# A gated recurrent cell on one core: half B's candidate for half A's chunks made in half A's bank, ten passes a step

## The chip, the cores and the metric

The kernel runs on one core of one Trainium2 chip. The metric is the device time of one execution in microseconds. Before the change it is 1663.17 us, the median of three runs (1661.68 to 1664.26). The engines are TensorE (PE, with its weight loads shown as PEld), VectorE (DVE), ScalarE (ACT), GpSimd (POOL) and the DMA queues, here issued by SyncE (SP).

## What is computed

A recurrent cell runs over 512 steps for a batch of 8, with 512 inputs and 512 units, all in 32-bit floats, and its states are added to the input:

```
def step(h, x_t):
    fused = sigmoid(concatenate([x_t, h], -1) @ w_W + w_b)
    hidden_state, output_state = split(fused, 2, -1)          # r and z
    memory_state = x_t @ wx_W + wx_b + hidden_state * (h @ wh_W + wh_b)
    h_new = output_state * h + (1 - output_state) * tanh(memory_state)
    return h_new, h_new
out = x + states
```

Each step needs the state of the step before, so nothing can be batched over time on the side of h: three products of the state (r, z and the candidate's h @ wh_W, called hh here) and then two sigmoids, a tanh and the update. The products of x don't depend on the state and are made ahead.

## The kernel before

**Layout.** Unit u lies on partition 32j + p in chunk c: four quads j of 128 units, each in four chunks of 32. Chunks 0 and 1 are half A, chunks 2 and 3 half B. The state of a step is the stationary operand of a product (32 columns: 8 batch rows of this step and zeros for three others of its group of four steps), the weights are the moving one. One *pass* is one chunk of the state against one bank's weights: four matrix products, one for each quad j, in four 32-wide strips of the array. Each fp32 product shows as two MATMUL records, so a pass has eight.

**Banks.** Products are added into PSUM tiles: A (192 columns: hh, z, r of half A), B (128: r, hh of half B), C (64: z of half B), each in two copies for alternate groups of four steps, and two tiles `xp` for the x side. Four steps share a bank; the rows of the other steps keep the x side and the biases, which `spread` (L254) copies in on ScalarE ahead of each group, from `xs` by the columns in `XP` (L43).

**A step** (loop at L363). PE takes the passes in the order of the string `ORDER` (L27): A0 B0 A1 A2 A3 B1 B2 B3 C0 C1 C2 C3, the digit being the chunk of the state. Passes 0 and 1 need half A's new state, 2 and 3 half B's. Then comes one part of the x products of a group that lies ahead (`products`, L293; an eighth each step, as much as one pass of 384 columns in four steps of a group of eight and of 288 in the other four; they end 12 steps before the last). The first step has its own order `FIRST` (L29), in which half A's bank is `xp` itself.

**VectorE and ScalarE in a step** (L458 to L483), in this order on each engine's queue: for half A `turn_r`, `turn_h`, `turn_z` (32x32 transposes out of PSUM, with a sigmoid on ScalarE behind r and z), `memory(0, q)` (a scan that makes r * hh + x, with a tanh behind it, one for each chunk q); then `turn_r(1)`, `turn_h(1)`, `update(0, 0)`, `turn_z(1)`, `update(0, 1)`, `memory(1, q)`, `update(1, q)`. `update` is a scan that makes z * h + (1 - z) * n, the new state, which the next step's weight loads wait for. `memory` scans over slots: `md0` holds [0, r], `md1` holds [hh, x], so a unit has two elements and the second result is the one wanted. Behind these stand copies and adds for the x side, different in each step of a group of eight (L487 to L547), and two tiny memsets. GpSimd adds the state to the input.

The order on each engine is written by hand (`manual_schedule`, L186); what waits for what follows from the tiles, with a few manual dependencies: the second update of half A waits for the sigmoid of half B's r (L467).

**Start.** SP brings wx (four parts), wa (four parts, by chunk of the state), wb (chunks 0 to 2, then 3), then the inputs.

Of the kernel before, what the change touches and what calls it, by code (L numbers as in the profile page):

```python
# [25 lines left out]

ORDER = "A0 B0 A1 A2 A3 B1 B2 B3 C0 C1 C2 C3"  # L27

FIRST = "A0 x A1 x A2 x A3 B0 B1 B2 B3 C0 C1 C2 C3"  # L29

BANKS = {"A": 192, "B": 128, "C": 64}

HALF = 192
# [5 lines left out]
Q01, Q23 = slice(0, 64), slice(64, 128)  # L39

COLS = slice(64, 448)

XP = {"A": slice(0, 192), "X": slice(192, 320), "C": slice(320, 384), "B": slice(384, 512)}  # L43


@with_exitstack
def tile_cond_rnn_residual(
# [5 lines left out]
    wa_d: bass.AP,  # L53
    wb_d: bass.AP,
    wb3_d: bass.AP,
    bias_d: bass.AP,
# [30 lines left out]
    nc = tc.nc  # L87
# [4 lines left out]
    const = ctx.enter_context(tc.tile_pool(name="const", bufs=1))  # L92
# [38 lines left out]

    wa = const.tile([P, NQ, NQ, 192], F32, name="wa")
    for k in range(NQ):
        nc.sync.dma_start(out=wa[:, k], in_=wa_d[k])
    wb = const.tile([P, NQ, NQ, 192], F32, name="wb")
    nc.sync.dma_start(out=wb[:, :3], in_=wb_d)
    nc.sync.dma_start(out=wb[:, 3], in_=wb3_d)

    def wh(bank, k, j):
        return wa[:, k, j] if bank == "A" else wb[:, k, j, {"C": slice(0, 64), "B": slice(64, 192)}[bank]]  # L140
# [9 lines left out]
    NH = 2 * GS  # L150
    hT = [[pair(n, f"hT{n}{i}", 32, 3) for i in range(NH)] for n in "AB"]

    md0 = [[pair(n, f"md0{n}{i}", 32, 2) for i in range(2)] for n in "AB"]
    md1 = [[pair(n, f"md1{n}{i}", 32, 2) for i in range(2)] for n in "AB"]
    hd0 = [[pair(n, f"hd0{n}{i}", B, 3) for i in range(2)] for n in "AB"]
# [10 lines left out]
    nc.scalar.activation(const.tile([P, 1], F32, name="table"), zeros[:, :1], AF.Sigmoid)  # L166
    for n, t_ in enumerate(hd0[0] + hd0[1] + md0[0] + md0[1] + hT[0] + hT[1]):
# [7 lines left out]
    step_bias = const.tile([P, HALF], F32, name="stepbias")  # L175
    xs = [const.tile([P, 512], F32, name=f"xs{n}") for n in range(2)]
    u2 = const.tile([P, WIDE], F32, name="u2")
# [3 lines left out]
    def state(hf, i, slot=2):  # L181

        s = i % GS
        return hT[hf][i % NH][:, B * s : B * s + B, :, slot]
# [8 lines left out]
    def mm(out_, lhsT, rhs, start=False):  # L193
        nc.tensor.matmul(  # L194
            out_, lhsT, rhs, start=start, stop=False, skip_group_check=True
        )
# [13 lines left out]
    for t_ in xs:  # L210
        for c_ in (slice(0, 64), slice(448, 512)):
            nc.gpsimd.tensor_copy(t_[:, c_], bias[:, c_])
    for hf in range(2):
# [9 lines left out]
    def act(key, out_, in_, func, **kw):  # L223
        inst = nc.scalar.activation(out_, in_, func, **kw).ins  # L224
# [24 lines left out]

    def source(g):  # L250

        return xs[g % 2] if g else xps[0]

    def spread(g, names):  # L254

        for n in names:
            nc.scalar.copy(banks[g % 2][n], source(g)[:, XP[n]])

    def turn_x(g, e):

        c0 = XP["X"].start + 32 * e
        nc.vector.transpose(md1[e // 2][g % 2][:, :, e % 2, 1], source(g)[:, c0 : c0 + 32])

# [92 lines left out]
    weight_sum(0)  # L356
    spread(0, "BCA")
    for e in range(NQ):
# [4 lines left out]
    for i in range(T):  # L363
        g, s = divmod(i, GS)
        c, t = divmod(i, TC)
        ps = banks[g % 2]
# [21 lines left out]
        def scan(c_, out_, d0, d1):  # L388
# [23 lines left out]
        def turn_r(hf):  # L412
            tr, _ = turned("r", hf)
            r_done[hf] = act(
                ("r", hf, g % 2, s),
                md0[hf][g % 2][:, rows, :, 1].rearrange("p n c -> p c n"),
                tr,
                AF.Sigmoid,
            )

        def turn_h(hf):
            inst = nc.vector.transpose(  # L422
                md1[hf][g % 2][:, :, :, 0].rearrange("p n c -> p c n"), raw["h"][hf]
            ).ins
            h_done[hf] = inst
            if hf == 0 and i + 1 - NH in pool_done:
                tc.add_manual_dep(inst, pool_done[i + 1 - NH].name, SYNC)

        def turn_z(hf):
# [10 lines left out]
            )  # L440

        ms = [
            work.tile([P, 2, B, 2], F32, tag=f"m{hf}", name=f"m{hf}_{i}").rearrange("p c n s -> p n c s")
            for hf in range(2)
        ]

        def memory(hf, q):

            c_ = slice(q, q + 1)
            scan(c_, ms[hf], md0[hf][g % 2][:, rows], md1[hf][g % 2][:, rows])  # L450
            act(("n", hf, q, i % NH), state(hf, i, 1)[:, :, c_], ms[hf][:, :, c_, 1], AF.Tanh)
# [37 lines left out]
        if i == 0:  # L489
            nc.scalar.copy(xs[1][:, COLS], xps[1][:, COLS])  # L490
            spread(1, "B")
            turn_x(1, 0)
        add_ = nc.vector.tensor_tensor
        if u == 3 and o and nxt:
            add_(xs[0][Q23, COLS], xps[0][Q23, COLS], both[Q23], ALU.add)
        elif u == 7 and two:
            nc.vector.tensor_copy(xs[0][Q01, COLS], xps[0][Q01, COLS])
        elif u == 0 and o and nxt:
            add_(u3[Q23], xps[1][Q23, COLS], u2[Q23], ALU.add)
# [4 lines left out]
        if u == 0:  # L504
            spread(2 * o + 1, "C")
            if o and nxt:
                nc.scalar.copy(xps[0][Q01, lo], step_bias[Q01])
                nc.scalar.copy(xps[1][Q23, lo], step_bias[Q23])
        elif u == 1:
            spread(2 * o + 1, "A")  # L510
            if o == 0:
                seed(3)
        elif u == 2:
            if o == 0:
                nc.scalar.copy(xs[0][:, COLS], xps[0][:, COLS])
            elif nxt:
                nc.scalar.copy(both[Q23, HALF:], xps[0][Q01, lo])
                nc.vector.tensor_copy(both[Q23, :HALF], xps[1][Q23, lo])
            if two:
                nc.scalar.copy(xps[0][Q01, COLS], bias[Q01, COLS])  # L520
        elif u == 3:
            if o == 0:
                nc.scalar.copy(xs[1][:, COLS], xps[1][:, COLS])
            if two:
                x_sum(o + 2, 2)
        elif u == 4 and nxt:
            if o:
                add_(xs[1][Q01, COLS], xps[1][Q01, COLS], u3[Q23], ALU.add)
            spread(2 * o + 2, "A")
            if two:  # L530
                x_sum(o + 2, 0)
        elif u == 5 and nxt:
            if o:
                add_(xs[1][Q23, COLS], u3[Q23], both[Q23], ALU.add)
            if two:
                nc.scalar.copy(xps[0][Q23, COLS], xps[0][Q01, COLS])
                x_sum(o + 2, 1)
            spread(2 * o + 2, "C")
        elif u == 6 and nxt:
            spread(2 * o + 2, "B")  # L540
            if two:
                nc.vector.memset(xps[1][Q01, COLS], 0.0)
                x_sum(o + 2, 3)
        elif u == 7 and nxt:
            if two:
                nc.scalar.copy(u2[Q23], xps[0][Q23, COLS])
            spread(2 * o + 3, "B")  # L547
        if i < len(SUMS):
# [108 lines left out]
```

## Time and profile before

| | |
|---|---|
| median of the runs | 1663.17 us |
| profiled execution, first to last instruction | 1659.2 us |
| PE, share busy | 99% |
| PEld, share busy | 89% |
| DVE | 78% |
| ACT | 67% |
| POOL | 20% |
| granted clock of TensorE | 1.000 |

In a group line or a row of the timeline, `L194 PE MATMUL A<-wa,hTA 128*32 128x192 f32 x8` means: line 194 of the kernel, on PE, writes tile A from the weights wa and the state of half A (hTA); 128 by 32 is stationary, 128 by 192 moving; eight records. In brackets stands how long the engine was idle before, and which instruction ended that. The names on VectorE are tr, tz (transposed r and z), md1A and md1B (transposed hh), m (the scan behind tanh), hTA and hTB (the state). Busy time of PE is made of pipelined records whose ends are modelled; differences of starts tell more.

### The profile page before, as it was taken

The numbers are of one execution on the slowest core, as the hardware profiler recorded it, in microseconds if no ns is written. First come the engines' busy times: TensorE is split into PE (matmuls) and PEld (weight loads), VectorE is DVE, ScalarE is ACT, GpSimd is POOL, SyncE is SP. The second block draws the span as 40 slices with busy tenths as digits, with TensorE's granted clock in tenths as the row PEclk, the third lists the DMA queues.
The fourth block names the chain that finished last, engine by engine and source line by source line (L and its number), as shares of the span: only waits on it lengthen the run. The fifth ranks groups of instructions, "written<-read, shape, count | busy, mean of one in ns | idle before, by whom it ended". The sixth has DMA issues, their size and how long they took to land.

```text
span 1659.2 us, 126037 instructions
## 1 busy us (share of the span) xinstructions
PE 1647.1 (99%) x54254; PEld 1484.3 (89%) x54254; DVE 1298.5 (78%) x9702; ACT 1106.9 (67%) x5884; POOL 325.6 (20%) x1284
## 2 busy tenths in 40 slices
PE   8999999999999999999999999999999999999998
PEld 5899999999999888899999999988899999999997
DVE  6877777777777777777777777777777777777776
ACT  4666666666666666666666666666666666666665
POOL 2221121211211212112112121121121211211211
PEclk9999999999999999999999999999999999999999
DMA  4000000000000000000000000000000000000000
GB/s 180 17 5 18 17 18 18 17 6 18 17 17 18 5 18 18 18 18 5 18 18 18 18 12 10 18 17 18 18 5 18 17 18 18 5 17 11 11 11 10
DMA packets 11512, 31.16 MB, mean 19 GB/s; under 512 B 1220, under 2 KB 1732, under 8 KB 10824
## 3 DMA queue, kind: packets, MB, share of 16 engines
q1 hardware_dynamic: 10800, 22.94, 4.0%
q8 instruction: 424, 6.95, 1.8%
q14 instruction: 136, 1.11, 0.2%
q10 hardware_dynamic: 152, 0.16, 0.0%
HBM read 14.70 MB, written 8.39 MB: 14 GB/s over the span
## 4 chain that ended last, share of the span: by engine, by line
PE 98%; DMA 1%; DVE 1%; issue 0%; ACT 0%; SPq 0%
PE A L194 40%; PE B L194 26%; PE xp L194 18%; PE C L194 13%; DMA wb<-in_wb_dram 1%; DMA wx<-in_wx_dram 0%; DVE tr L406 0%; DVE m L390 0%; DVE tz L406 0%; DVE hTA L390 0%; DVE md1A L422 0%; DVE md1B L422 0%; ACT hTB L224 0%; SPq L130 0%; DVE hTB L390 0%
## 5 line engine op out<-in xcount | busy, mean ns | idle before, releaser
L194 PE MATMUL A<-wa,hTA 128*32 128x192 f32 x8176 | 555.5, 327 | 2.7 <-DVE hTA L390 2.7
L194 PE MATMUL B<-wb,hTA 128*32 128x128 f32 x8192 | 453.0, 273 | 0.9 <-DMA wb<-in_wb_dram 0.9
L194 PE MATMUL A<-wa,hTB 128*32 128x192 f32 x8176 | 446.6, 326 | 0.0
L194 PEld LDWEIGHTS A<-wa,hTA 128*32 128x32 f32 x8176 | 290.7, 122 | 128.4 <-DVE hTA L390 107.1
L558 POOL TENSOR_TENSOR ot<-xin,hTB 128x16 f32<-128x16 f32 x503 | 125.6, 250 | 1292.4 <-DVE hTB L390 1281.8
L194 PEld LDWEIGHTS B<-wb,hTA 128*32 128x32 f32 x8192 | 346.8, 122 | 10.8 <-DMA wb<-in_wb_dram 1.3
L194 PE MATMUL B<-wb,hTB 128*32 128x128 f32 x8192 | 338.6, 273 | 0.1
L194 PEld LDWEIGHTS A<-wa,hTB 128*32 128x32 f32 x8176 | 324.3, 122 | 15.5 <-DVE hTB L390 0.3
L224 ACT ACTIVATE md0A<-tr 128x16 f32<-128x16 f32 x512 | 112.3, 219 | 314.4 <-DVE tr L406 314.4
L406 DVE STREAM_TRANSPOSE tr<-A 128x64 f32<-128x64 f32 x511 | 127.7, 250 | 214.3 <-PE A L194 199.3
L194 PE MATMUL xp<-tw,sx 128*32 128x384 f32 x1984 | 274.2, 406 | 0.3 <-issue 0.3
L194 PEld LDWEIGHTS B<-wb,hTB 128*32 128x32 f32 x8192 | 261.1, 122 | 0.4 <-DMA wb<-in_wb_dram 0.4
L390 DVE TENSOR_TENSOR_SCAN hTB<-hd0B,hTB 128x24 f32<-128x24 f32 x1024 | 157.8, 195 | 100.5 <-ACT hTB L224 100.5
L194 PE MATMUL C<-wb,hTB 128*32 128x64 f32 x8192 | 230.0, 219 | 0.1
L194 PE MATMUL C<-wb,hTA 128*32 128x64 f32 x8192 | 229.1, 219 | 0.0
L194 PE MATMUL xp<-wx,xin 128*32 128x384 f32 x1056 | 210.1, 486 | 0.0
L194 PEld LDWEIGHTS C<-wb,hTA 128*32 128x32 f32 x8192 | 206.6, 122 | 0.0
L390 DVE TENSOR_TENSOR_SCAN hTA<-hd0A,hTA 128x24 f32<-128x24 f32 x1024 | 190.9, 186 | 0.0
L194 PEld LDWEIGHTS C<-wb,hTB 128*32 128x32 f32 x8192 | 179.5, 122 | 0.6 <-issue 0.4
L224 ACT ACTIVATE hd0B<-tz 128x16 f32<-128x16 f32 x512 | 115.7, 226 | 94.8 <-DVE tz L406 94.8
L224 ACT ACTIVATE hTB<-hTB 128x16 f32<-128x16 f32 x512 | 120.1, 235 | 79.2 <-DVE hTB L390 70.3
L224 ACT ACTIVATE hTA<-m 128x8 f32<-128x8 f32 x1024 | 160.8, 206 | 2.5
(98 smaller groups left out, 2710.0 us busy)
## 6 DMA issues: line engine op xcount, KB each, us to landing
xin<-in_x_dram SPq DMA_DIRECT2D x31, 256.0 KB, 3.3
out_dram<-ot SPq DMA_DIRECT2D x31, 256.0 KB, 2.1
wx<-in_wx_dram SPq DMA_DIRECT2D x4, 768.0 KB, 7.1
wa<-in_wa_dram SPq DMA_DIRECT2D x4, 384.0 KB, 9.1
wb<-in_wb_dram SPq DMA_DIRECT2D x1, 1152.0 KB
wb<-in_wb_dram SPq DMA_DIRECT2D x1, 384.0 KB, 11.2
out_dram<-ot SPq DMA_DIRECT2D x1, 192.0 KB, 2.1
head<-in_xh_dram ACTq DMA_DIRECT2D x1, 144.0 KB, 5.0
```

The lines of the kernel that those rows point to most:

```text
L194: nc.tensor.matmul(out_, lhsT, rhs, start=start, stop=False, skip_group_check=True)
L224: inst = nc.scalar.activation(out_, in_, func, **kw).ins
L390: return nc.vector.tensor_tensor_scan(*[t_[:, :, c_].rearrange("p n c s -> p (n c s)") for t_ in (out_, d0, d1)], 0.0, ALU.mult, ALU.add,).ins
L406: inst = nc.vector.transpose(t_.rearrange("p c n -> p (c n)"), raw[n][hf]).ins
L558: return engine.tensor_tensor(ot[:, t, 2 * hf : 2 * hf + 2, :].rearrange("p c n -> p n c"), x_of(c, slice(2 * hf, 2 * hf + 2), t, 1).rearr ...
```

## The change

The columns a step multiplies stay the same, but they lie in other banks. Bank A has 256 columns, of which the first 64 are hh of half B; for chunks 0 and 1 the pass takes all 256, for chunks 2 and 3 the last 192. Bank D (128) holds z and r of half B. Bank H (64) holds hh of half B for chunks 2 and 3 alone. So a step has ten passes. The two parts of hh of half B are added in the scan: `md1` of half B has three slots [part, H, x], `md0` of half B [0, 1, r], and `turn_part` is a new transpose on VectorE of A's first 64 columns. `update(0, 0)` moves ahead of `turn_h(1)`. Half A's first 64 columns start at zero, from a widened `xs`; biases and x parts move to the new columns.

```diff
-ORDER = "A0 B0 A1 A2 A3 B1 B2 B3 C0 C1 C2 C3"
-FIRST = "A0 x A1 x A2 x A3 B0 B1 B2 B3 C0 C1 C2 C3"
-BANKS = {"A": 192, "B": 128, "C": 64}
+ORDER = "A0 A1 A2 A3 D0 D1 D2 D3 H2 H3"
+FIRST = "A0 x A1 x A2 x A3 D0 D1 D2 D3 H0 H1 H2 H3"
+BANKS = {"A": 256, "D": 128, "H": 64}
...
-XP = {"A": slice(0, 192), "X": slice(192, 320), "C": slice(320, 384), "B": slice(384, 512)}
+XP = {"A": slice(0, 256), "X": slice(256, 384), "D": slice(384, 512), "H": slice(512, 576)}
...
-    wa = const.tile([P, NQ, NQ, 192], F32, name="wa")
+    wa = const.tile([P, NQ, NQ, 256], F32, name="wa")
...
-    wb = const.tile([P, NQ, NQ, 192], F32, name="wb")
-    nc.sync.dma_start(out=wb[:, :3], in_=wb_d)
-    nc.sync.dma_start(out=wb[:, 3], in_=wb3_d)
+    wd = const.tile([P, NQ, NQ, 128], F32, name="wd")
+    nc.sync.dma_start(out=wd[:, :3], in_=wd_d)
+    nc.sync.dma_start(out=wd[:, 3], in_=wd3_d)
...
+    for t_ in md0[1]:
+        nc.gpsimd.memset(t_[:, :, :, 1], 1.0)
...
             hs = hT[k // 2][i % NH][:, :, k % 2, 2]
+            to, w_ = {
+                "A": (ps["A"], wa) if k < 2 else (ps["A"][:, 64:], wa[:, :, :, 64:]),
+                "D": (ps["D"], wd),
+                "H": (ps["H"], wa[:, :, :, :64]),
+            }[bank]
+            if bank == "A" and i == 0:
+                to, w_ = xps[0][:, :HALF], wa[:, :, :, 64:]
             for j in range(NQ):
-                to = ps[bank] if i or bank != "A" else xps[0][:, XP["A"]]
-                mm(to[32 * j : 32 * j + 32, :], hs, wh(bank, k, j))
+                mm(to[32 * j : 32 * j + 32, :], hs, w_[:, k, j])
...
-        pa = ps["A"] if i else xps[0][:, XP["A"]]
+        pa = ps["A"][:, HU:] if i else xps[0][:, :HALF]
         raw = {
-            "h": (pa[:, :HU], ps["B"][:, HU:]),
-            "z": (pa[:, HU : 2 * HU], ps["C"]),
-            "r": (pa[:, 2 * HU :], ps["B"][:, :HU]),
+            "h": (pa[:, :HU], ps["H"]),
+            "z": (pa[:, HU : 2 * HU], ps["D"][:, :HU]),
+            "r": (pa[:, 2 * HU :], ps["D"][:, HU:]),
         }
...
+        def turn_part():
+            nc.vector.transpose(md1[1][g % 2][:, :, :, 0].rearrange("p n c -> p c n"), ps["A"][:, :HU])
+
         ms = [
-            work.tile([P, 2, B, 2], F32, tag=f"m{hf}", name=f"m{hf}_{i}").rearrange("p c n s -> p n c s")
+            work.tile([P, 2, B, 2 + hf], F32, tag=f"m{hf}", name=f"m{hf}_{i}").rearrange("p c n s -> p n c s")
...
         memory(0, 1)
+        if i:
+            turn_part()
         turn_r(1)
+        update(0, 0)
         turn_h(1)
-        update(0, 0)
         turn_z(1)
         tc.add_manual_dep(update(0, 1), r_done[1].name, SYNC)
...
         if u == 0:
-            spread(2 * o + 1, "C")
+            spread(2 * o + 1, "D")
...
-            spread(2 * o + 2, "C")
+            spread(2 * o + 2, "D")
         elif u == 6 and nxt:
-            spread(2 * o + 2, "B")
+            spread(2 * o + 2, "H")
...
-            spread(2 * o + 3, "B")
+            spread(2 * o + 3, "H")
```

More of the change, by code (lines that the diff above doesn't have):

```diff
@@ L41 @@
 COLS = slice(64, 448)
-XP = {"A": slice(0, 192), "X": slice(192, 320), "C": slice(320, 384), "B": slice(384, 512)}
+SC = slice(128, 512)
+XP = {"A": slice(0, 256), "X": slice(256, 384), "D": slice(384, 512), "H": slice(512, 576)}
 @with_exitstack
@@ L53, in tile_cond_rnn_residual @@
     wa_d: bass.AP,
-    wb_d: bass.AP,
-    wb3_d: bass.AP,
+    wd_d: bass.AP,
+    wd3_d: bass.AP,
     bias_d: bass.AP,
@@ L130, in tile_cond_rnn_residual @@
         nc.sync.dma_start(out=wx[:, k], in_=wx_d[k])
-    wa = const.tile([P, NQ, NQ, 192], F32, name="wa")
+    wa = const.tile([P, NQ, NQ, 256], F32, name="wa")
     for k in range(NQ):
         nc.sync.dma_start(out=wa[:, k], in_=wa_d[k])
-    wb = const.tile([P, NQ, NQ, 192], F32, name="wb")
-    nc.sync.dma_start(out=wb[:, :3], in_=wb_d)
-    nc.sync.dma_start(out=wb[:, 3], in_=wb3_d)
-    def wh(bank, k, j):
-        return wa[:, k, j] if bank == "A" else wb[:, k, j, {"C": slice(0, 64), "B": slice(64, 192)}[bank]]
+    wd = const.tile([P, NQ, NQ, 128], F32, name="wd")
+    nc.sync.dma_start(out=wd[:, :3], in_=wd_d)
+    nc.sync.dma_start(out=wd[:, 3], in_=wd3_d)
     load_x(0, 1)
@@ L151, in tile_cond_rnn_residual @@
     hT = [[pair(n, f"hT{n}{i}", 32, 3) for i in range(NH)] for n in "AB"]
-    md0 = [[pair(n, f"md0{n}{i}", 32, 2) for i in range(2)] for n in "AB"]
-    md1 = [[pair(n, f"md1{n}{i}", 32, 2) for i in range(2)] for n in "AB"]
+    md0 = [[pair(n, f"md0{n}{i}", 32, m) for i in range(2)] for n, m in (("A", 2), ("B", 3))]
+    md1 = [[pair(n, f"md1{n}{i}", 32, m) for i in range(2)] for n, m in (("A", 2), ("B", 3))]
     hd0 = [[pair(n, f"hd0{n}{i}", B, 3) for i in range(2)] for n in "AB"]
@@ L166, in tile_cond_rnn_residual @@
     nc.scalar.activation(const.tile([P, 1], F32, name="table"), zeros[:, :1], AF.Sigmoid)
-    for n, t_ in enumerate(hd0[0] + hd0[1] + md0[0] + md0[1] + hT[0] + hT[1]):
+    for n, t_ in enumerate(hd0[0] + hd0[1] + md0[0] + md0[1] + hT[0] + hT[1] + md1[1]):
         (nc.vector if n < DVE_FILL else nc.gpsimd).memset(t_, 0.0)
+    for t_ in md0[1]:
+        nc.gpsimd.memset(t_[:, :, :, 1], 1.0)
     for t_ in hd0[0] + hd0[1]:
@@ L175, in tile_cond_rnn_residual @@
     step_bias = const.tile([P, HALF], F32, name="stepbias")
-    xs = [const.tile([P, 512], F32, name=f"xs{n}") for n in range(2)]
+    xs = [const.tile([P, 576], F32, name=f"xs{n}") for n in range(2)]
     u2 = const.tile([P, WIDE], F32, name="u2")
@@ L210, in tile_cond_rnn_residual @@
     for t_ in xs:
-        for c_ in (slice(0, 64), slice(448, 512)):
-            nc.gpsimd.tensor_copy(t_[:, c_], bias[:, c_])
+        nc.gpsimd.memset(t_[:, :64], 0.0)
+        nc.gpsimd.tensor_copy(t_[:, 64:128], bias[:, :64])
+        nc.gpsimd.tensor_copy(t_[:, 512:], bias[:, 448:])
     for hf in range(2):
@@ L248, in prefill_two, with source @@
         yield from prefill(3)
-    def source(g):
-        return xs[g % 2] if g else xps[0]
+    def source(g, c0, c1):
+        return xs[g % 2][:, c0:c1] if g else xps[0][:, c0 - 64 : c1 - 64]
     def spread(g, names):
         for n in names:
-            nc.scalar.copy(banks[g % 2][n], source(g)[:, XP[n]])
+            skip = 64 if n == "A" and not g else 0
+            nc.scalar.copy(banks[g % 2][n][:, skip:], source(g, XP[n].start + skip, XP[n].stop))
     def turn_x(g, e):
         c0 = XP["X"].start + 32 * e
-        nc.vector.transpose(md1[e // 2][g % 2][:, :, e % 2, 1], source(g)[:, c0 : c0 + 32])
+        nc.vector.transpose(md1[e // 2][g % 2][:, :, e % 2, 1 + e // 2], source(g, c0, c0 + 32))
     def wx_of(kh, nh):
@@ L356, in tile_cond_rnn_residual @@
     weight_sum(0)
-    spread(0, "BCA")
+    spread(0, "HDA")
     for e in range(NQ):
@@ L415, in turn_r @@
                 ("r", hf, g % 2, s),
-                md0[hf][g % 2][:, rows, :, 1].rearrange("p n c -> p c n"),
+                md0[hf][g % 2][:, rows, :, 1 + hf].rearrange("p n c -> p c n"),
                 tr,
@@ L422, in turn_h @@
             inst = nc.vector.transpose(
-                md1[hf][g % 2][:, :, :, 0].rearrange("p n c -> p c n"), raw["h"][hf]
+                md1[hf][g % 2][:, :, :, hf].rearrange("p n c -> p c n"), raw["h"][hf]
             ).ins
@@ L450, in memory @@
             scan(c_, ms[hf], md0[hf][g % 2][:, rows], md1[hf][g % 2][:, rows])
-            act(("n", hf, q, i % NH), state(hf, i, 1)[:, :, c_], ms[hf][:, :, c_, 1], AF.Tanh)
+            act(("n", hf, q, i % NH), state(hf, i, 1)[:, :, c_], ms[hf][:, :, c_, 1 + hf], AF.Tanh)
         def update(hf, q):
@@ L489, in tile_cond_rnn_residual @@
         if i == 0:
-            nc.scalar.copy(xs[1][:, COLS], xps[1][:, COLS])
-            spread(1, "B")
+            nc.scalar.copy(xs[1][:, SC], xps[1][:, COLS])
+            spread(1, "H")
             turn_x(1, 0)
@@ L494, in tile_cond_rnn_residual @@
         if u == 3 and o and nxt:
-            add_(xs[0][Q23, COLS], xps[0][Q23, COLS], both[Q23], ALU.add)
+            add_(xs[0][Q23, SC], xps[0][Q23, COLS], both[Q23], ALU.add)
         elif u == 7 and two:
-            nc.vector.tensor_copy(xs[0][Q01, COLS], xps[0][Q01, COLS])
+            nc.vector.tensor_copy(xs[0][Q01, SC], xps[0][Q01, COLS])
         elif u == 0 and o and nxt:
@@ L514, in tile_cond_rnn_residual @@
             if o == 0:
-                nc.scalar.copy(xs[0][:, COLS], xps[0][:, COLS])
+                nc.scalar.copy(xs[0][:, SC], xps[0][:, COLS])
             elif nxt:
@@ L522, in tile_cond_rnn_residual @@
             if o == 0:
-                nc.scalar.copy(xs[1][:, COLS], xps[1][:, COLS])
+                nc.scalar.copy(xs[1][:, SC], xps[1][:, COLS])
             if two:
@@ L527, in tile_cond_rnn_residual @@
             if o:
-                add_(xs[1][Q01, COLS], xps[1][Q01, COLS], u3[Q23], ALU.add)
+                add_(xs[1][Q01, SC], xps[1][Q01, COLS], u3[Q23], ALU.add)
             spread(2 * o + 2, "A")
@@ L533, in tile_cond_rnn_residual @@
             if o:
-                add_(xs[1][Q23, COLS], u3[Q23], both[Q23], ALU.add)
+                add_(xs[1][Q23, SC], u3[Q23], both[Q23], ALU.add)
             if two:
@@ L626 @@
     wx_d = chunks(cat((z[:D], half_a), (r[:D], half_a), (wxm, both), (z[:D], half_b), (r[:D], half_b)))
-    wa_d = chunks(cat((whm, half_a), (z[D:], half_a), (r[D:], half_a)))
-    wb = units(cat((z[D:], half_b), (r[D:], half_b), (whm, half_b)))
-    wb_d, wb3_d = c_(wb[:, :3]), c_(wb[:, 3])
+    wa_d = chunks(cat((whm, half_b), (whm, half_a), (z[D:], half_a), (r[D:], half_a)))
+    wd = units(cat((z[D:], half_b), (r[D:], half_b)))
+    wd_d, wd3_d = c_(wd[:, :3]), c_(wd[:, 3])
     rb, zb = wb_[:512], wb_[512:]
@@ L643 @@
     for name, a in (
-        ("x", xd), ("xh", xh_d), ("wx", wx_d), ("wa", wa_d), ("wb", wb_d), ("wb3", wb3_d), ("bias", bias_d),
+        ("x", xd), ("xh", xh_d), ("wx", wx_d), ("wa", wa_d), ("wd", wd_d), ("wd3", wd3_d), ("bias", bias_d),
     ):
```

## The prediction

> **What bounds the kernel now.** I read the page first, then the table of waits, then the timeline of one ordinary step.
>
> ```profile
> span 1659.2 us, 126037 instructions
> PE 1647.1 (99%) x54254; PEld 1484.3 (89%) x54254; DVE 1298.5 (78%) x9702; ACT 1106.9 (67%) x5884; POOL 325.6 (20%) x1284
> ```
>
> ```profile
> PEld A L194 <- DVE hTA L390: 107.1, 379, 0.5
> ...
> PE A L194 <- DVE hTA L390: 2.7, 11, 0.3
> ```
>
> TensorE is busy throughout. Its weight loads wait 107 us for VectorE's new state, but its products only 2.7 us: the state arrives just in time, behind other products. So the time is the sum of the passes, plus whatever the state becomes late by. The passes, on PE (time of first start, length, count; a length overlaps the next, so I use differences of starts):
>
> ```profile
> 798.20 0.86 PE L194 MATMUL A<-wa,hTB 128*32 128x192 f32 x16
> 798.85 0.43 PE L194 MATMUL B<-wb,hTA 128*32 128x128 f32 x8
> 799.07 0.65 PE L194 MATMUL B<-wb,hTB 128*32 128x128 f32 x16
> 799.51 0.43 PE L194 MATMUL C<-wb,hTA 128*32 128x64 f32 x16
> 799.73 0.43 PE L194 MATMUL C<-wb,hTB 128*32 128x64 f32 x16
> 799.96 0.41 PE L194 MATMUL xp<-tw,xin 128*32 128x288 f32 x2
> ...
> 800.44 0.54 PE L194 MATMUL A<-wa,hTA 128*32 128x192 f32 x8
> 800.77 0.43 PE L194 MATMUL B<-wb,hTA 128*32 128x128 f32 x8
> 800.98 0.54 PE L194 MATMUL A<-wa,hTA 128*32 128x192 f32 x8
> 801.31 0.86 PE L194 MATMUL A<-wa,hTB 128*32 128x192 f32 x16
> ...
> 803.06 0.49 PE L194 MATMUL xp<-wx,xin 128*32 128x384 f32 x2
> ...
> 803.71 0.54 PE L194 MATMUL A<-wa,hTA 128*32 128x192 f32 x8
> ```
>
> Eight records are one pass. Two passes of 192 columns take 0.65 (798.20 to 798.85), so 0.325 each; four of 64 take 0.45 (799.51 to 799.96), so 0.1125 each; one of 128 takes 0.22. A line through these is 1.66 ns a column and 6 ns a pass. The x products at a step's end take 0.48 in a short step (799.96 to 800.44) and 0.65 in a long one (803.06 to 803.71).
>
> ```profile
> L194 PE MATMUL xp<-wx,sx 128*32 128x288 f32 x496 | 83.2, 406 | 0.0
> ```
>
> A group of eight steps has 8 such records, so there are 62 groups, and by `products` each has four short and four long steps: 248 of each. Around the same steps VectorE runs:
>
> ```profile
> 799.12 0.25 DVE L406 STREAM_TRANSPOSE tr<-A 128x64 f32<-128x64 f32 x1 [0.37 <-PE A L194]
> 799.29 0.21 DVE L422 STREAM_TRANSPOSE md1A<-A 128x64 f32<-128x64 f32 x1
> ...
> 799.85 0.23 DVE L406 STREAM_TRANSPOSE tr<-B 128x64 f32<-128x64 f32 x1
> 800.00 0.21 DVE L422 STREAM_TRANSPOSE md1B<-B 128x64 f32<-128x64 f32 x1
> 800.13 0.20 DVE L390 TENSOR_TENSOR_SCAN hTA<-hd0A,hTA 128x24 f32<-128x24 f32 x1
> 800.25 0.22 DVE L406 STREAM_TRANSPOSE tz<-C 128x64 f32<-128x64 f32 x1
> 800.39 0.17 DVE L390 TENSOR_TENSOR_SCAN hTA<-hd0A,hTA 128x24 f32<-128x24 f32 x1
> 800.48 0.25 DVE L390 TENSOR_TENSOR_SCAN m<-md0B,md1B 128x16 f32<-128x16 f32 x2
> 800.93 0.31 DVE L390 TENSOR_TENSOR_SCAN hTB<-hd0B,hTB 128x24 f32<-128x24 f32 x2 [0.20 <-ACT hTB L224]
> 801.27 0.56 DVE L495 TENSOR_TENSOR xs<-xp,both 64x384 f32<-64x384 f32 x1
> 801.87 0.21 DVE L262 STREAM_TRANSPOSE md1A<-xs 128x32 f32<-128x32 f32 x1
> 802.03 0.07 DVE L556 MEMSET idle<- 128x1 f32 x2
> 802.22 0.25 DVE L406 STREAM_TRANSPOSE tr<-A 128x64 f32<-128x64 f32 x1
> ```
>
> Bank A is finished at 798.85; its first transpose starts 0.27 later. From there half A's new state is due to A0 (scan 800.13, product 800.44), half B's to A2 (scan 800.93, product 801.31). What a late state costs stands at the end of the program, where 12 steps have no x product to wait behind; the first row is the load of A2's weights in the step above:
>
> ```profile
> 801.19 0.61 PEld L194 LDWEIGHTS A<-wa,hTB 128*32 128x32 f32 x16
> ...
> 1642.87 0.20 DVE L390 TENSOR_TENSOR_SCAN hTA<-hd0A,hTA 128x24 f32<-128x24 f32 x1
> ...
> 1643.13 0.19 PEld L194 LDWEIGHTS A<-wa,hTA 128*32 128x32 f32 x8 [0.39 <-DVE hTA L390]
> ```
>
> ```profile
> 1643.13 0.55 PE L194 MATMUL A<-wa,hTA 128*32 128x192 f32 x8 [0.24 <-DVE hTA L390]
> 1643.49 0.40 PE L194 MATMUL B<-wb,hTA 128*32 128x128 f32 x8
> ...
> 1646.21 0.55 PE L194 MATMUL A<-wa,hTA 128*32 128x192 f32 x8 [0.24 <-DVE hTA L390]
> ```
>
> The load starts 0.26 after its scan starts (1642.87, 1643.13). With nothing to hide it, the pass takes 0.36 (to 1643.49) and not 0.325: an uncovered load costs 0.04. In the ordinary short step A2's load comes 0.26 after the scan too (800.93, 801.19) and 0.12 ahead of its product. So half B has 0.12 - 0.04 = 0.08 us to spare in a short step and, with x products 0.17 longer, 0.25 in a long one.
>
> **The change part by part.** *Passes.* C0 and C1 go into A0 and A1; C0 to C3 and B0 to B3 become D0 to D3, H2 and H3. Columns a step stay 1536, passes fall from twelve to ten. At 6 ns a pass that is 12 ns a step, over 511 steps 6.1 us. The trace has no 256-column pass in 32-wide strips: bounded below by columns alone (0.425), above by a 192 and a 64 put together (0.4375); I take the line, 0.43.
>
> *VectorE's order.* Added: a transpose of A's first 64 columns, ahead of tr of half B. Transposes of this shape cost from start to next start 0.13 (800.00 to 800.13), 0.15 (799.85 to 800.00) or 0.17 (799.12 to 799.29). By the row that also writes md1B: 0.13. But r and z now share bank D, and D3 ends four 0.22 passes after A3, not three: tr of half B can't start before 0.87 + 0.27 after bank A's end, 0.87 after tr of half A, where it started 0.73 after it (799.12, 799.85). Both reasons give the same place, 0.13 to 0.14 later, so the floor is 0.14 even if the added transpose were free, and the ceiling 0.17. The scan of half A's state trades places with the second transpose, so it keeps its place (two transposes ahead of it before, two now): half A is due at A0 as before, 0.01 at risk. The transpose of H waits for H3, 0.87 + 0.22 = 1.09 after tr of half A; its place in the queue is 1.14, so no wait. Behind these stand z's transpose, the second scan of half A (needed at A1, now 0.43 after A0; it lands in time) and both m scans of half B, all 0.14 later.
>
> *Wider scans.* Half B's two m scans go from 16 to 24 elements. Two of 24 take 0.31 together (800.93), two of 16 0.25 (800.48), but one of 24 alone takes 0.17 (800.39). Bounds 0 to 0.05 on the way to tanh; I take 0.01.
>
> *Half B's deadline.* From A3's end to A2 there were ten passes and the x products, now eight: the two saved passes lie in this stretch, so A2 is due 0.012 earlier. Lateness: 0.14 + 0.01 + 0.012 - 0.08 = about 0.08 in a short step; I take 0.07, since a short step already holds some 0.01 of half A's waiting, which this one swallows. In a long step 0.25 - 0.16 = 0.09 is left: no stall.
>
> The Trainium skill, "TensorE: Matmul & The Clock Gate", section "LDWEIGHTS (loading the stationary operand)", puts a load at its columns divided by 1.2 in ns, an estimate of 27 ns for these 32 columns against the 0.04 of the rows above. By that rule each stall is 13 ns shorter and the sum below 3.2 us lower, 1674.0. The rows decide here.
>
> *Sum.* Stalls 248 x 0.07 = +17.4. Passes -6.1. In one short step of each group an add of 0.56 and a transpose stand between half B's scans and the next tr of half A, as at 801.27 to 802.22; 800.93 to 802.22 is 1.29 against A2-bound 0.26 + 0.04 + 0.65 + 0.27 = 1.22. That row waits for bank A almost as long itself, so I take 0.02 of the 0.07: 62 x 0.02 = +1.2. At the end 11 steps go from 3.08 (1643.13 to 1646.21, half A's loop) to half B's loop, 0.27 + 1.81 + 0.15 + 0.30 + 0.65 = 3.18: +1.1, and the 0.1 counted for their passes comes back: +1.2. Start-up:
>
> ```profile
> 17.88 0.66 PE L194 MATMUL B<-wb,hTA 128*32 128x128 f32 x16 [0.93 <-DMA wb<-in_wb_dram]
> ```
>
> ```profile
> 1.16 6.45 DMA wx<-in_wx_dram
> 7.63 11.19 DMA wb<-in_wb_dram
> ```
>
> The queue brings 6144 KB of weights by 18.8, about 350 KB a us. The first recurrent pass outside A waited for 1536 + 1152 KB behind wx; now for 2048 + 768, 128 KB more: +0.3. Scalar copies into the banks widen for A by 64 columns and swap 64 and 128 elsewhere; they lie behind ScalarE's wait:
>
> ```profile
> 799.40 0.22 ACT L224 ACTIVATE md0A<-tr 128x16 f32<-128x16 f32 x1 [0.16 <-DVE tr L406]
> ```
>
> That is the fullest step, with 0.16 left; half B's shift takes 0.15, the later tr gives 0.07 back: nothing, and at most 0.1 in one step of eight (6 us) if this cover fails. GpSimd's adds end no chain. In all +17.4 - 6.1 + 1.2 + 1.2 + 0.3 = +14.0: 1659.2 + 14.0 = 1673.2 in the profile's span. The median of the runs, 1663.17, lies 4.0 above that span: 1677.2.
>
> **The rivals.** (1) *Half B's state stays in time*: only the passes count, 1663.2 - 6.1 + 0.3 = 1657.4. For it: VectorE idles 0.37 ahead of tr (799.12), and ScalarE has room. Against: that idle lies behind half B's scans, not ahead of them. It decides from a lateness under 0.025 a short step (6.1 / 248). Chance 0.11. (2) *The stall is there but nearly paid for*: the load hides itself (0.04 off), 0.03 a stall, 7.4 - 6.1 + 2.7 = +4.0 at the most, +1.6 if the end and the adds cost nothing: 1665 to 1667. Chance 0.10, six tenths of it under 1666.5. (3) *A wide pass costs its two parts*, the change doesn't save passes: +6.1, 1683.3. The straight line through three widths speaks against it. Chance 0.06. (4) *VectorE is slower than its rows*: transpose 0.17, scans 0.05: 0.08 more on 248 steps, +19.8, 1697.0. Chance 0.06; each alone gives about 1687.
>
> **How the numbers follow.** The forecast has 0.67, with 1669 to 1687 as its own range (stall 0.04 to 0.11). To hold eight in ten I reach down over rival 2 to 1664; up, 1687 takes in rival 3 and either half of rival 4. About 0.2% is what a measurement of this kernel can tell from no change, 1659.8 to 1666.5: faster 0.11, same 0.06, slower 0.83.
>
> **What would show it.** In the profile after: passes of A with 256 columns 0.43 apart; half B's first state scan 1.95 to 1.97 after tr of half A, not 1.81; waits of A<-hTB on VectorE's hTB in about half of the steps, on PE and not on its loads alone; short steps of 3.16 to 3.18, long ones of 3.25 (now 3.27). It is wrong if A2 shows no wait, if A0 waits more than A2, if long steps stall as well, or if tr of half B starts where it did.

## The result, and the profile after

The kernel after takes 1681.45 us, the median of four runs (1681.36 to 1681.52), beside 1662.43 for the kernel before (1661.25 to 1664.26): a ratio of 1.0113, with a 95% interval of 1.0101 to 1.0125. It is slower, as forecast, and inside the range. By the two profiled executions the gap is 20.5 us (1679.7 against 1659.2), where the forecast had 14.0; the runs of the kernel before happen to scatter upward from its span more than those after.

The page's first lines for the kernel after:

```profile
span 1679.7 us, 110201 instructions
...
PE 1667.8 (99%) x46078; PEld 1237.3 (74%) x46078; DVE 1402.8 (84%) x10213; ACT 1190.5 (71%) x5884; POOL 327.2 (19%) x1290
```

TensorE has 8176 records fewer and is as "busy" as before. That share is useless here: it stays at 99% although, as shown below, products wait for their weight loads for 28.8 us in all; the profile counts such a product as running. The table of waits of the same kernel hides it as well (engine, line, waited for: us, times, longest):

```profile
PEld A L195 <- DVE hTA L399: 171.3, 644, 0.8
PEld A L195 <- DVE hTB L399: 145.6, 509, 0.5
```

Weight loads waited for half B's state once before, for 0.3 us, and now in nearly every step; but the loads run ahead of the products, so most of its 145.6 us is covered, and no row for products on hTB exists. The stall has to be read from starts. The timeline of the kernel after on PE, from a short step's x products to the next short step:

```profile
799.57 0.41 PE L195 MATMUL xp<-tw,xin 128*32 128x288 f32 x2
...
800.05 1.05 PE L195 MATMUL A<-wa,hTA 128*32 128x256 f32 x16
800.99 0.87 PE L195 MATMUL A<-wa,hTB 128*32 128x192 f32 x16
801.68 0.62 PE L195 MATMUL D<-wd,hTA 128*32 128x128 f32 x16
802.11 0.62 PE L195 MATMUL D<-wd,hTB 128*32 128x128 f32 x16
802.55 0.41 PE L195 MATMUL H<-wa,hTB 128*32 128x64 f32 x16
802.77 0.25 PE L195 MATMUL xp<-tw,xin 128*32 128x96 f32 x2
...
803.26 0.61 PE L195 MATMUL A<-wa,hTA 128*32 128x256 f32 x8
```

A0 and A1 take 0.94 before A2 starts, and A2 and A3 0.69 (800.99 to 801.68), not 0.65: A2 waits, and then pays for an uncovered load. The step lasts 3.21 (800.05 to 803.26). VectorE around the same place:

```profile
798.72 0.25 DVE L415 STREAM_TRANSPOSE tr<-A 128x64 f32<-128x64 f32 x1 [0.35 <-PE A L195]
...
799.25 0.28 DVE L399 TENSOR_TENSOR_SCAN m<-md0A,md1A 128x16 f32<-128x16 f32 x2
799.45 0.26 DVE L452 STREAM_TRANSPOSE md1B<-A 128x64 f32<-128x64 f32 x1
799.60 0.24 DVE L415 STREAM_TRANSPOSE tr<-D 128x64 f32<-128x64 f32 x1
799.76 0.17 DVE L399 TENSOR_TENSOR_SCAN hTA<-hd0A,hTA 128x24 f32<-128x24 f32 x1
799.85 0.26 DVE L431 STREAM_TRANSPOSE md1B<-H 128x64 f32<-128x64 f32 x1
800.00 0.21 DVE L415 STREAM_TRANSPOSE tz<-D 128x64 f32<-128x64 f32 x1
800.13 0.21 DVE L399 TENSOR_TENSOR_SCAN hTA<-hd0A,hTA 128x24 f32<-128x24 f32 x1
800.26 0.28 DVE L399 TENSOR_TENSOR_SCAN m<-md0B,md1B 128x24 f32<-128x24 f32 x2
800.72 0.31 DVE L399 TENSOR_TENSOR_SCAN hTB<-hd0B,hTB 128x24 f32<-128x24 f32 x2 [0.18 <-ACT hTB L226]
```

From tr of half A (798.72) tr of half B starts 0.88 later (before 0.73), half A's first scan 1.04 (1.01), half B's m 1.54 (1.36), half B's first state scan 2.00 (1.81). Medians over steps 16 to 489 of each trace are 2.009 and 1.814.

To compare steps I took the difference between the first starts of A0 in consecutive steps, and its median for each of the eight kinds of step (60 of each). Before, short steps last 3.105 to 3.110 and long ones 3.265. After, a step in which A2 doesn't wait lasts 3.095 or 3.255. Four of each eight wait: three short ones (3.218, 3.213, 3.205) and the first long one (3.367, where the state comes out of a short step). So the mean stall is 0.116.

### The profile page after: what moved, and what is told of

It is laid out like the page before. It is cut to its first block, busy times and chain, and to the rows that moved or that the text cites. A ratio compares the mean times of both kernels' runs of the same rounds, so it can differ in the third digit from the quotient of the medians.

```text
span 1679.7 us, 110201 instructions
## 1 busy us (share of the span) xinstructions
PE 1667.8 (99%) x46078; PEld 1237.3 (74%) x46078; DVE 1402.8 (84%) x10213; ACT 1190.5 (71%) x5884; POOL 327.2 (19%) x1290
## 4 chain that ended last, share of the span: by engine, by line
PE 97%; DVE 2%; DMA 1%; ACT 0%; issue 0%
PE A L195 48%; PE D L195 26%; PE xp L195 17%; PE H L195 7%; DMA wd<-in_wd_dram 1%; DVE tr L415 0%; DMA rows<-in_bias_dram 0%; DVE m L399 0%; DVE md1B L452 0%; DVE tw L283 0%; DVE tz L415 0%; DVE md1A L431 0%; DVE hTA L399 0%; DVE hTB L399 0%; ACT hTB L226 0%
## 5 line engine op out<-in xcount | busy, mean ns | idle before, releaser
L195 PE MATMUL A<-wa,hTA 128*32 128x256 f32 x8176 | 535.3, 379 | 3.0 <-DVE hTA L399 3.0
L195 PEld LDWEIGHTS A<-wa,hTB 128*32 128x32 f32 x8176 | 250.8, 123 | 165.8 <-DVE hTB L399 145.4
L195 PE MATMUL D<-wd,hTA 128*32 128x128 f32 x8192 | 317.6, 273 | 1.2 <-DMA wd<-in_wd_dram 1.2
L195 PE MATMUL D<-wd,hTB 128*32 128x128 f32 x8192 | 317.5, 273 | 0.0
L195 PEld LDWEIGHTS D<-wd,hTA 128*32 128x32 f32 x8192 | 257.2, 122 | 22.2 <-DMA wd<-in_wd_dram 1.5
L195 PEld LDWEIGHTS D<-wd,hTB 128*32 128x32 f32 x8192 | 240.4, 122 | 0.0
L195 PE MATMUL H<-wa,hTB 128*32 128x64 f32 x8192 | 208.2, 219 | 0.0
L195 PEld LDWEIGHTS H<-wa,hTB 128*32 128x32 f32 x8192 | 185.5, 122 | 0.0
L226 ACT ACTIVATE hTB<-m 128x8 f32<-128x8 f32 x1024 | 163.8, 208 | 4.4
L399 DVE TENSOR_TENSOR_SCAN m<-md0A,md1A 128x16 f32<-128x16 f32 x1024 | 142.2, 181 | 8.8
```

The source lines that it names most:

```text
L195: nc.tensor.matmul(out_, lhsT, rhs, start=start, stop=False, skip_group_check=True)
L399: return nc.vector.tensor_tensor_scan(*[t_[:, :, c_].rearrange("p n c s -> p (n c s)") for t_ in (out_, d0, d1)], 0.0, ALU.mult, ALU.add,).ins
```

## The experiments

Theory S is the prediction's: half B's state comes later because of where its r is turned and what VectorE does behind it, and A2 waits for it. In the tables and texts below a place in the step is counted in us from tr of half A, as a median over the steps. Behind each time stands its range; each ratio, with its 95% interval in brackets, is against runs of the kernel before taken together with it, whose medians lie from 1660.17 to 1661.33.

**1. Without the added transpose.** From the kernel after:

```diff
-        if i:
-            turn_part()
```

> The changed kernel without the added transpose (turn_part); hh of half B for half A's chunks is left out of the result. Theory S (half B's state is late because bank D ends a pass later AND because of the added transpose, each enough by itself): tr of half B stays 0.87 us after tr of half A, held by D's end; short steps stay at 3.20 to 3.21 us and the time at 1679 to 1682. Rival Q (VectorE's queue alone makes it late): tr of half B goes back to 0.73, half B's first state scan to 1.86 from 2.00, the short steps to 3.10, the time to 1656 to 1660.

1681.59 us (1681.48 to 1681.78), ratio 1.0128 [1.0111, 1.0145]. Nothing changes: tr of half B at 0.873, half B's first scan at 2.009. The transpose stood in time in which VectorE would have waited for bank D anyway.

**2. The added transpose alone, in the kernel before**, with half A's first scan moved ahead of the update's transpose as in the change. Bank D isn't there, and there are twelve passes:

```diff
+        if i:
+            nc.vector.transpose(spare[:, :, :, 0].rearrange("p n c -> p c n"), ps["A"][:, :HU])
         turn_r(1)
+        update(0, 0)
         turn_h(1)
-        update(0, 0)
```

> The kernel before with nothing changed on TensorE: twelve passes, but on VectorE one more transpose of A's first 64 columns into a spare tile, and the order of half A's update as in the change. Theory S: half B's first state scan moves from 1.81 to 1.95 to 1.97 us after tr of half A, short steps stall by 0.06 to 0.11, the time is 1676 to 1690. Rival P (the wide passes or their loads make the change slow): nothing is wide here, 1660 to 1665.

1670.57 (1670.49 to 1671.35), ratio 1.0062 [1.0047, 1.0077]: slower, but less than expected. The place is as in the change (tr of half B 0.882) and the same four steps stall, by 0.04, since the state comes at 1.947 and not at 2.009.

**3. The 256-column passes as 64 and 192**, twelve passes again:

```diff
-            for j in range(NQ):
-                mm(to[32 * j : 32 * j + 32, :], hs, w_[:, k, j])
+            wide = bank == "A" and k < 2 and i > 0
+            for c0, c1 in ((0, HU), (HU, 256)) if wide else ((0, to.shape[1]),):
+                for j in range(NQ):
+                    mm(to[32 * j : 32 * j + 32, c0:c1], hs, w_[:, k, j, c0:c1])
```

> The changed kernel with each 256-column pass issued as 64 and 192 columns: twelve passes again. Theory S: short steps are bound by half B's loop and stay at 3.20 to 3.22 us; long steps grow by 0.01 to 3.265; 3 us more, 1684 to 1685, and up to 4 us beyond that if the scattered short stalls of TensorE seen in the profile before (46 steps, 4.3 us, none after) come from the number of its instructions. Rival P (a wide pass has a cost of its own): the time falls to 1670 or less.

1686.1 (1685.67 to 1687.1), ratio 1.0156 [1.014, 1.0171]. Steps that don't wait go from 3.255 back to 3.265; those that wait hardly move (3.218 to 3.220, 3.213 to 3.211), since they are set by half B's state. So a pass saved is worth 5 ns, and only where nothing waits.

**4. Half B's first memory scan ahead of half A's second update**, in the kernel after:

```diff
         turn_z(1)
+        memory(1, 0)
         tc.add_manual_dep(update(0, 1), r_done[1].name, SYNC)
...
-        memory(1, 0)
```

> The changed kernel with the first m scan of half B put ahead of the second state scan of half A on VectorE. Theory S: that scan starts 1.42 us after tr of half A, not 1.53, when the sigmoid of r is done; half B's first state scan at 1.90, not 2.00; short steps 3.11 to 3.13, the time 1658 to 1664. If the second half of A's state then comes too late for A1: 0.02 to 0.05 more a short step, 1664 to 1672. Rival P: no change, 1681.

1703.35 (1702.76 to 1703.79), ratio 1.0258 [1.0243, 1.0274]: a miss. On VectorE:

```profile
801.17 0.30 DVE L431 STREAM_TRANSPOSE md1B<-H 128x64 f32<-128x64 f32 x1
801.31 0.20 DVE L415 STREAM_TRANSPOSE tz<-D 128x64 f32<-128x64 f32 x1
801.57 0.21 DVE L399 TENSOR_TENSOR_SCAN m<-md0B,md1B 128x24 f32<-128x24 f32 x1
801.69 0.18 DVE L399 TENSOR_TENSOR_SCAN hTA<-hd0A,hTA 128x24 f32<-128x24 f32 x1
```

The scan doesn't start 0.14 after z's transpose, but 0.26 (801.31 to 801.57; median place 1.51): its inputs, from the update's transpose and from ScalarE's sigmoid of r, both end at 1.38 to 1.41. Half A's second scan stands behind the wait and comes at 1.636, not 1.422, so A1 is late too (0.51 behind A0, not 0.43) and even long steps stall (3.30 to 3.33). So there is a second floor under m, its inputs, about 1.5 in this kernel. Step by step the trace tells the two inputs apart: in nine steps of ten m starts 0.102 to 0.104 after the end of the update's transpose, but anything from 0.10 to 0.21 after the end of the sigmoid. In this order the transpose holds it.

**5. Without the added transpose, and with two slots** in half B's memory tiles:

```diff
-    md0 = [[pair(n, f"md0{n}{i}", 32, m) for i in range(2)] for n, m in (("A", 2), ("B", 3))]
+    md0 = [[pair(n, f"md0{n}{i}", 32, 2) for i in range(2)] for n in "AB"]
```

(and so for `md1` and `ms`)

> The changed kernel without the added transpose and with two slots, not three, in half B's scans (hh of half B for half A's chunks is left out of the result). Theory S with bank D's end as the hold: tr of half B stays at 0.87 us after tr of half A and the scan of half A's state at 1.05; only what the third slot costs comes off, 0.02 to 0.04 of half B's first state scan (2.01 to 1.97 to 1.99), so 1672 to 1678. If the slots cost nothing: 1681. Rival Q (VectorE's queue): 1660 or less.

1673.99 (1673.77 to 1674.12), ratio 1.0076 [1.0063, 1.009]. Beside run 1 that is 7.6 us for the third slot. m comes at 1.534 instead of 1.544, the state at 1.979 instead of 2.009: 0.03, not the 0.01 of the prediction. The stall falls with it, from 0.116 to 0.087.

**6. Bank D ready early.** D2 and D3 directly behind A3, and D0 and D1 last into columns that nothing reads, so z and r of half B are made without half A's chunks:

```diff
-ORDER = "A0 A1 A2 A3 D0 D1 D2 D3 H2 H3"
+ORDER = "A0 A1 A2 A3 D2 D3 H2 H3 E0 E1"
-BANKS = {"A": 256, "D": 128, "H": 64}
+BANKS = {"A": 384, "D": 128, "H": 64}
...
+                "E": (banks[1 - g % 2]["A"][:, 256:], wd),
```

> The changed kernel with the passes in the order A0 A1 A2 A3 D2 D3 H2 H3 and then D0 and D1 into columns that nobody reads (z and r of half B lack half A's chunks in the result; TensorE's work is the same). Bank D ends 0.44 us earlier; the added transpose stays. Theory S: tr of half B stays at 0.88 because of the added transpose alone, but waits for nothing; half A's scan goes from 1.05 back to 1.02, half B's first state scan to 1.95 to 1.98; short steps 3.15 to 3.18; 1669 to 1675. If D's end alone were the cause: no stall, 1650 to 1657.

1671.19 (1670.95 to 1671.48), ratio 1.006 [1.0046, 1.0073]. tr of half B still starts at 0.881, now held by the added transpose ahead of it. Only its wait is gone, and with it 0.035 behind it (half A's first scan at 1.013, not 1.047).

**7. Bank D early and no added transpose.** Run 6 without `turn_part()`.

> As the run before, and without the added transpose: both reasons for the lateness gone, the ten passes kept (hh, z and r of half B lack half A's chunks). Theory S: tr of half B at 0.73, half B's first state scan at 1.83 to 1.87, no stall in any step: short 3.095, long 3.255; 5 us under the kernel before for the passes and up to 4 more for the scattered stalls of TensorE: 1650 to 1656. Rival P (TensorE's side has a cost of its own): 1660 or more.

1668.03 (1667.82 to 1668.17), ratio 1.0041 [1.0025, 1.0056]: a miss. Both things that S named were gone, and it still stalled. VectorE in this run:

```profile
798.82 0.25 DVE L416 STREAM_TRANSPOSE tr<-A 128x64 f32<-128x64 f32 x1 [0.77 <-PE A L195]
...
799.55 0.23 DVE L416 STREAM_TRANSPOSE tr<-D 128x64 f32<-128x64 f32 x1
799.82 0.21 DVE L400 TENSOR_TENSOR_SCAN hTA<-hd0A,hTA 128x24 f32<-128x24 f32 x1
799.95 0.25 DVE L432 STREAM_TRANSPOSE md1B<-H 128x64 f32<-128x64 f32 x1
800.10 0.21 DVE L416 STREAM_TRANSPOSE tz<-D 128x64 f32<-128x64 f32 x1
800.23 0.17 DVE L400 TENSOR_TENSOR_SCAN hTA<-hd0A,hTA 128x24 f32<-128x24 f32 x1
800.32 0.28 DVE L400 TENSOR_TENSOR_SCAN m<-md0B,md1B 128x24 f32<-128x24 f32 x2
800.78 0.31 DVE L400 TENSOR_TENSOR_SCAN hTB<-hd0B,hTB 128x24 f32<-128x24 f32 x2 [0.19 <-ACT hTB L226]
```

tr of half B is back at 0.73. But half A's first scan starts 0.27 behind it and not 0.13: it needs the tanh of half A, which ScalarE ends at 0.975 (median), so it can't start before 1.01. In the kernel before the update's transpose stands in that hole, for free. The change put it behind the scan, so three instructions, not two, lie between 1.01 and half B's m: 1.497, not 1.37. S had left out the swap.

**8. The change in half of the steps.** The groups of four that are long steps run as in the change, the others and the last twelve steps as before, with a weight tile of its own for the wide passes:

```diff
+def wide(g):
+    return g % 2 == 1 and g < 125
...
-        for n in (ORDER if i else FIRST).split():
+        wd_ = wide(g)
+        for n in (WIDE_ORDER if wd_ else ORDER if i else FIRST).split():
```

> Long steps as in the change (ten passes, wide bank, three slots), short steps and the last 12 as before (twelve passes). Theory S: half B's lateness of about 0.2 us fits into the 0.25 that it has to spare in a long step, so nothing stalls: short steps 3.105 to 3.11, long ones 3.255, not 3.265; 2.6 us less than the kernel before and up to 2 more for scattered stalls, a ratio of 0.997 to 0.999. If the lateness spills over: above 1.000.

1659.63 (1657.19 to 1662.06, eleven runs), ratio 0.9989 [0.9981, 0.9998]: the one version that computes the whole cell and is faster than the kernel before, by 0.1% (about 2 us), with an interval that barely leaves out 1. In its long steps half B's state comes as late as in the change (2.005), and still none of them stalls: they last 3.255. By the step medians that is 2.5 us; against it the second step starts at 22.41 instead of 20.21, with 1024 KB more of weights to load at the start.

**9. Run 7 with the swap undone:**

```diff
-        update(0, 0)
         turn_h(1)
+        update(0, 0)
```

> The run with bank D's end early and no added transpose, with one more thing put back: VectorE turns half B's update (md1B from H) ahead of half A's first hTA scan, as before.py has it, and not behind it. Half A's part of z, r and hh of half B is left out of the output, as in that run. Theory S (amended): in that run tr of half B was back at 0.73 us after tr of half A, but the update's transposes stood behind the scan, which itself waits for ScalarE's tanh until 1.01, so three VectorE instructions (0.36 us and more) lay between 1.01 and half B's m (1.50) and not two (1.37 before). With the update turned in the scan's wait, m of half B comes at 1.36 to 1.41, the first hTB scan at 1.81 to 1.87, A2 waits no more, the steps are 3.095 and 3.255, and the time is 1650 to 1657 (ratio 0.993 to 0.998). Rival W: the width itself (three slots, 192-column passes of half B) holds half B's state; then the time stays at 1664 to 1669 and hTB at 1.93 or later.

1651.66 (1651.36 to 1651.84), ratio 0.9946 [0.9928, 0.9964]: 16.4 us less than run 7, for the place of one transpose. VectorE and then PE in this run:

```profile
798.47 0.23 DVE L416 STREAM_TRANSPOSE tr<-D 128x64 f32<-128x64 f32 x1
798.62 0.25 DVE L432 STREAM_TRANSPOSE md1B<-H 128x64 f32<-128x64 f32 x1
798.75 0.20 DVE L400 TENSOR_TENSOR_SCAN hTA<-hd0A,hTA 128x24 f32<-128x24 f32 x1
798.88 0.22 DVE L416 STREAM_TRANSPOSE tz<-D 128x64 f32<-128x64 f32 x1
799.02 0.18 DVE L400 TENSOR_TENSOR_SCAN hTA<-hd0A,hTA 128x24 f32<-128x24 f32 x1
799.12 0.28 DVE L400 TENSOR_TENSOR_SCAN m<-md0B,md1B 128x24 f32<-128x24 f32 x2
799.58 0.31 DVE L400 TENSOR_TENSOR_SCAN hTB<-hd0B,hTB 128x24 f32<-128x24 f32 x2 [0.19 <-ACT hTB L226]
```

```profile
799.23 1.05 PE L195 MATMUL A<-wa,hTA 128*32 128x256 f32 x16
800.10 0.83 PE L195 MATMUL A<-wa,hTB 128*32 128x192 f32 x16
800.75 0.62 PE L195 MATMUL D<-wd,hTB 128*32 128x128 f32 x16
```

The transpose fits between tr and the scan, which keeps its 0.28 (798.47 to 798.75). A0 and A1 take 0.87 and A2 and A3 0.65, with no wait. Steps last 3.095 to 3.100 and 3.255.

**10. Run 9 with two slots**, edited as in run 5.

> The run just before it with half B's update and memory tiles two slots wide and not three; the same parts are left out of the output. Theory S: where nothing is late the third slot costs nothing, since its 0.03 us on half B's state fall into time that A2 has left; the time is within 2 us of the run with three slots. Where the third slot still holds half B's state the time falls by 3 to 8 us, as it did between the kernel after without the part (1681.6) and the same with two slots (1674.0).

1651.59 (1651.33 to 1651.89), ratio 0.9946 [0.993, 0.9961]. The state comes at 1.815, not 1.840, and the time doesn't move: the same third slot that cost 7.6 us in run 5 is free where nothing is late.

**The places in one table.** Places and stalls are medians from the traces; the stall is the mean over the four kinds of step that wait, against 3.095 and 3.255 (runs 2 and 3, with twelve passes: 3.105, 3.110 and 3.265). Run 4 is left out, since A1 waits there too.

| kernel | tr of half B | r's sigmoid ends | m of half B | first hTB scan | stall | scan less stall |
|---|---|---|---|---|---|---|
| before | 0.730 | 1.210 | 1.368 | 1.814 | 0 | |
| 2 | 0.882 | 1.343 | 1.501 | 1.947 | 0.041 | 1.906 |
| after | 0.882 | 1.387 | 1.544 | 2.009 | 0.116 | 1.893 |
| 1 | 0.873 | 1.387 | 1.544 | 2.009 | 0.117 | 1.892 |
| 3 | 0.882 | 1.386 | 1.543 | 2.009 | 0.105 | 1.904 |
| 5 | 0.873 | 1.377 | 1.534 | 1.979 | 0.087 | 1.892 |
| 6 | 0.881 | 1.348 | 1.505 | 1.970 | 0.075 | 1.895 |
| 7 | 0.730 | 1.218 | 1.497 | 1.957 | 0.064 | 1.893 |
| 9 | 0.731 | 1.218 | 1.375 | 1.840 | 0 | |
| 10 | 0.731 | 1.210 | 1.370 | 1.815 | 0 | |

The last column is the deadline: half B's first scan may start 1.893 after tr of half A with ten passes, and some 0.012 later with twelve. All ten-pass kernels that stall lie within 0.002 of the one line "stall = scan - 1.893"; 9 and 10 come earlier than that and don't stall.

The columns before it tell what holds m. In every kernel of the table except run 7, the median step has m 0.157 or 0.158 after the sigmoid's end, wherever the sigmoid lies. In run 7 the sigmoid is early and m is held by VectorE's queue, 0.217 behind z's transpose.

## Why the prediction was right, and where its size was off

**Half B's deadline** was right almost to the digit. The prediction had 0.08 to spare at 1.81 and took 0.012 off for the passes: 1.88; the table says 1.893. The pattern too: long steps don't stall, except the first one behind short ones. The uncovered load of 0.04 shows again in A2 and A3 (0.69 beside run 9's 0.65). The Trainium skill ("TensorE: Matmul & The Clock Gate", section "LDWEIGHTS (loading the stationary operand)") puts a load at its columns divided by 1.2 in ns, an estimate of 27 ns for these 32 columns; the trace doesn't agree, and the measured 0.04 stands.

***VectorE's order* is the step that was mis-sized**, with *Wider scans*. Half B's state was put 0.15 later (0.14 and 0.01); it came 0.195 later. The prediction followed VectorE's queue from tr of half B to m. In the kernel after, m is held on another path: half A's second scan, which stands right ahead of m, has to wait for ScalarE's sigmoid of half B's r (a manual dependency that is named with the kernel before and that the prediction put at nothing), and m itself reads what the sigmoid writes. This sigmoid before and after, in the steps shown:

```profile
800.11 0.22 ACT L224 ACTIVATE md0B<-tr 128x16 f32<-128x16 f32 x1
```

```profile
799.88 0.23 ACT L226 ACTIVATE md0B<-tr 128x16 f32<-128x16 f32 x1
```

It ends at 800.33 and 800.11, and m starts 0.15 later both times (800.48 and 800.26). Over the steps of the kernel after, m starts 0.155 to 0.158 behind the sigmoid's end in nine of ten, while its distance from z's transpose goes from 0.23 to 0.27. By VectorE's queue alone it would start 0.217 behind z's transpose, as in run 7: at 1.50, not 1.544. In the kernel before both paths give the same place, 1.37, so nothing showed there.

Along this path the 0.195 comes apart like this: tr of half B 0.152 later (0.14 forecast); from tr to the sigmoid's end 0.505, not 0.480; from there to m the same; from m to the state 0.465, not 0.446. Of the last two, 0.025 and 0.019, the third slot makes 0.030 (run 5 beside run 1: 0.010 up to the sigmoid's end, 0.020 behind m), where *Wider scans* had 0.01. The other 0.014 isn't taken apart; tr's wait for bank D has a part in it, since in run 6, where tr starts at the same place without that wait, the sigmoid ends 0.467 behind it and not 0.505.

"Both reasons give the same place" was true and not the whole. Bank D's end and the added transpose cover each other (run 1 takes one away and gains nothing; run 6 takes the other away and keeps tr at 0.881). Under both lies a third, the swapped update transpose: with it VectorE's queue holds m at 1.50 however early the sigmoid ends (run 7), and only with the swap undone as well is m back at 1.37 (run 9). In the kernel after, the sigmoid's 1.544 lies above that floor, so undoing the swap alone should gain nothing. It couldn't be undone there without more changes either, since bank H ends 0.22 behind bank D, at 1.09 by the prediction's sum, when half A's scan is already due; that was not tried.

***Sum*, term by term.** By the step medians a group of eight takes 25.862 after and 25.490 before: 0.372 x 62 = +23.1. Stalls alone are 4 x 0.116 x 62 = +28.8, where the prediction had 17.4; the adds' extra 1.2 doesn't show as a step of its own. Passes give back 10 ns a step that doesn't wait (3.265 to 3.255, and run 3 undoes it), 5.1 us in all, where 6.1 was forecast. (Two of the three short kinds that wait would last 3.100 and not 3.095, as run 9 shows; counted from there the stalls are 28.1, and 28.1 less 5.0 for the passes is the 23.1.) The 11 last steps go from 3.08 to 3.21, +1.4 (forecast 3.18, +1.2). Start-up: the second step starts 0.35 earlier, not 0.3 later, but the kernels with the same loads scatter from 19.74 to 20.28, so this term isn't shown either way. And a term that the prediction didn't have: 46 steps of the kernel before lie over 15 ns above the median of their kind, 4.3 us in all, and no step of the kernel after does. 23.1 + 1.4 - 0.35 - 4.3 = 19.9 of the 20.5; the rest isn't assigned. The span was forecast 6.5 us too low, the time only 4.2 (1681.45 against 1677.2), and that difference is luck: the prediction carried over 4.0 us between span and median, and the kernel after has 1.8.

**The rivals.** (1) and (2) needed a state hardly late; it was later than forecast. (3) is out: a 256-column pass takes 0.432 (run 9's pair 0.87), on the straight line through 192 (0.325), 128 (0.218) and 64. (4) had the right direction, 0.045 where 0.08 was the rival's price, but only in part its reason: tr of half B came 0.012 later than forecast and the third slot cost 0.020 more, while the other 0.014 lies between tr and the end of ScalarE's sigmoid. The sign that A2's wait would show on PE's products was wrong; it shows in starts and on the loads alone.

## What to carry to other kernels

Ask of a queue not only what is added to it, but which instruction stood in a hole for free, and whether the change moves that one out: here, once bank D came early, one transpose behind a scan that waits anyway, or in front of it, was 16 us. Where three causes cover each other, taking away one shows nothing or little; find the deadline instead (scan less stall), which was the same within 0.003 in all ten-pass kernels that stall, and look for the path that holds the state: here a wait on another engine that was just covered before. And a cost of 0.03 us a step is 7.6 us or nothing, depending on whether the state it delays is already late, so the same edit can be kept where there is slack (the long steps, run 8) and left out where there is none.

## What was not expected of the hardware

TensorE has scattered gaps with nothing to wait for. In the kernel before, one of them on PE:

```profile
486.92 0.33 PE L194 MATMUL xp<-tw,sx 128*32 128x192 f32 x1
487.49 0.37 PE L194 MATMUL xp<-tw,sx 128*32 128x192 f32 x4 [0.25 <-issue]
```

That step takes 0.42 more than its kind. Kernels with twelve passes have 16 to 46 such steps (runs 3 and 2: 1.4 and 3.1 us; before 4.3), those with ten 0 to 14 (run 4 the most, 2.7 us). Stalls don't take them away by themselves, since runs 2 and 3 stall and have them, and ten passes do without any stall (runs 9 and 10 have none). Run 4 has ten passes and 14 such steps, so the number of PE's instructions isn't the whole reason, and the cause stays open. Run 8, with ten passes in half of its steps, has 38 (4.7 us).

A transpose into every third element takes longer than one into every second. After, by groups, and before:

```profile
L431 DVE STREAM_TRANSPOSE md1B<-H 128x64 f32<-128x64 f32 x512 | 140.9, 275 | 0.1
```

```profile
L422 DVE STREAM_TRANSPOSE md1B<-B 128x64 f32<-128x64 f32 x512 | 109.9, 215 | 0.0
```

The 275 ns against 215 are not all due to this, because the place in the queue changed too. Where only the slots differ, the same group has 274 ns against 235 (runs 1 and 5) and 244 against 218 (runs 9 and 10). The next instruction starts no later: z's transpose comes 0.148 behind it in run 1 and 0.147 in run 5.
